# Key, query and gate weights in one load each, zeros in threes, x reordered by a copy in memory: an AdaLN block with a delta-rule attention on one core

## The chip, the cores and the metric

The kernel runs on one core of one Trainium2 chip. The metric is the device time of one execution, in microseconds; the time of a kernel is the median of its runs. The profiled execution is one run of its own, taken by the hardware profiler, and its time is given beside the runs.

The names in the profile: PE is TensorE (PEld its weight loads), DVE is VectorE, ACT is ScalarE, POOL is GpSimd, SP is the engine that here only issues DMAs; SPq, PEq and so on are the issuing sides. L610 is line 610 of the kernel.

## What is computed

The block has two halves. The first is an attention without softmax over 4 sequences of 1024 tokens with 256 channels: 16 heads of 64, a causal convolution of 4 taps, and a state S of 64x64 per head and sequence that is carried from token to token. The second is a mixture of 8 experts of which every token takes 2. The reference, cut:

```python
q, k, v = (silu(causal_conv(x @ W.T)) for W in (Wq, Wk, Wv))      # 1024 channels
k = k / max(norm(k), 1e-12)                                        # per head
alpha, beta = sigmoid(x @ Wa.T + ba), sigmoid(x @ Wb.T + bb)
def step(S, xs):                                                   # token after token
    kt, vt, qt, at, bt = xs
    upd = vt - at * (S @ kt)
    S = clip(at * S + bt * outer(upd, kt), -5.0, 5.0)
    return S, S @ qt
out = (y * silu(x @ Wg.T + bg)) @ Wo.T

mod = (silu(c) @ wmod)                                             # six modulations
h = layernorm(x) * (1 + ca) + sa
x = x + ga * attention(h)
h = layernorm(x) * (1 + cb) + sb
x = x + gb * moe(h)                                                # top 2 of 8 experts
```

All arrays are float32.

## The kernel before

**Tiling.** The 1024 tokens of each sequence are cut into 32 chunks of 32 tokens; a chunk with all 4 sequences is 128 rows. Two chunks make a pair, and there are 16 pairs. Within a chunk the recurrence is solved in closed form (a triangular system per head), and S is carried from chunk to chunk. After the last pair, `blocks` runs the experts over blocks of 256 routed rows.

**What one turn of the main loop does** (`chunks`, lines 1505 to 1521). While the two chunks of pair g go through the passes with the state (`Chunk.passes`, L1098), pair g + 1 is prepared (`Pair`, from L640): rows and norms, decays, keys and queries, values and gates, the triangle, the scaling. Each of these is a generator, and the string `PLAN` says which generator takes its next step. So the order of the instructions on PE, DVE, ACT and POOL is written out by hand. SP's order is not: it is left to the scheduler, which places each DMA. Each engine works through its list in order; an instruction waits for semaphores, and all that stand behind it on its engine wait too.

**The instructions around the change, in the order in which data goes through them:**

- `load_kq` (L425): the weights of one head pair, a tile `w_kq` of keys and queries, by two DMAs of 128 KB on SP. `load_v` (L431): `w_v` by one DMA of 128 KB, and the gate's weights `w_gt` by two of 64 KB. They are called two head pairs ahead (L746, L771), and PE's projections L610 and L780 read them.
- `load_x` and `fill_x` (L417, L421): a chunk of x comes in an order (half, sequence, token) and is put into (sequence, half, token) by eight DMAs of 16 KB. `loads` (L1391) does this for two chunks a pair, three pairs ahead; the first two chunks are split between SP's and ACT's queues, and `later_loads` (L1472) fetches four more.
- `clear` (L1335): the rows in memory to which the routing will scatter are blanked, 132 KB (128 rows of 1056 bytes) by a DMA, in six steps of three a pair.
- `triangle` (L840): DVE turns the products of keys round (L871), takes from their diagonal the norms (`rk`, L874, L892) and from these and the decays the factors `spread` (L894, L895). SP stores them to `g_scratch` in memory (L900), four DMAs, one for each sequence's 32 partitions. Then DVE solves the triangular system: L920 and L926 for the blocks of 8, and for each of two halves L934, L941, L943, L948, L956. Of these L934, L943 and L948 are products of two operands in SBUF, L941 and L956 are reductions. Then Tt, Tn and r_r are turned (L962, L965, L967), and PE's L1019 reads Tn. In the plan, steps of other generators lie between: the routing (L541 to L583), the state's sum S (L1196), the projections' convolution (L628), the sum of the residual `add` (L1276).
- `scaled` (L978): four times (for keys w = 1 and for queries w = 0, and for both chunks `par`), SP loads a tile `sc` back from `g_scratch` by two DMAs, each of which broadcasts 4 KB to 64 partitions; POOL multiplies keys or queries by it in two instructions (L1001), and for the keys copies the last column to `last` (L1004). The four tiles share two buffers, which the triangle used before.
- POOL's list around it: the residual's sum x (L1278, which waits for DVE's L1276), the first multiply L1001, two indirect stores of the routing (L586, which wait for DVE's L583), `aS` (L1231, the state times its decay), two small copies into hT (L1070, L1091), the second multiply L1001, `last`, the third, `Tr` (L972), the fourth.
- DVE's S (L1196) reads `aS`; `yT` (L1252) follows S on DVE, and PE's next projection takes the bank that `yT` read.

The lines of the fan-out and of the read-back:

```python
for b, q in enumerate(quads):
    nc.sync.dma_start(g_dram[g][:, :, b].rearrange("w n t -> n w t"), spread[q])
...
def at_heads(g, w, p, par):
    n = p * 16 + par * 8
    return g_dram[g][w, n : n + 8].rearrange("n b t -> (n b t)")
```

Of the kernel before, what the change touches and what calls it, by code (L numbers as in the profile page):

```python
# [32 lines left out]
F32 = mybir.dt.float32  # L33
# [3 lines left out]
ALU = mybir.AluOpType  # L37
# [324 lines left out]
def chunks(ctx, tc, a, nch, con, ones, modt, modc, x1_dram, rt, out):  # L362
# [61 lines left out]

    def load_kq(hp):  # L425
        w = s3.tile([P, 2, 2, P], F32, name="w_kq")
        for x, i in ((KK, 0), (QC, 1)):
            nc.sync.dma_start(w[:, :, i], a["w_qkv"][:, :, x, hp])
        return w

    def load_v(hp):  # L431
        w = s3.tile([P, 2, P], F32, name="w_v", bufs=3)
        nc.sync.dma_start(w, a["w_qkv"][:, :, VC, hp])
        wg = s3.tile([P, 2, P], F32, name="w_gt", bufs=4)
        for p in range(2):
            nc.sync.dma_start(wg[:, :, half_p(p)], a["w_g"][:, :, p, hp * DH : (hp + 1) * DH])
        return w, wg
# [202 lines left out]
    class Pair:  # L640
# [100 lines left out]
        def keys_and_queries(self):  # L741
            need(("h", self.g), ("halo", self.g))
            kq = self.kq = take(s2, [P, 2, HP, 2, B, TC], "kq", bufs=2)
            for hp in range(HP):
# [3 lines left out]
                for x, i in ((KK, 0), (QC, 1)):  # L748
                    two.append(project(w[:, :, i], self.h_t, x, hp, kq[:, i, hp]))
                    yield  # L750
# [89 lines left out]
        def triangle(self):  # L840
# [58 lines left out]
            for b, q in enumerate(quads):  # L899
                nc.sync.dma_start(g_dram[g][:, :, b].rearrange("w n t -> n w t"), spread[q])  # L900
# [77 lines left out]
        def scaled(self):  # L978
# [11 lines left out]
            for w in (1, 0):  # L990
                for par in range(2):
                    sc = take(s1, [P, HP, B, TC], "sc", tag=("kk", "kk_r")[par])
                    for p in range(2):
                        nc.sync.dma_start(
                            sc[half_p(p)].rearrange("q h b t -> q (h b t)"),
                            at_heads(g, w, p, par).partition_broadcast(DH),
                        )
                    yield
                    for h4 in range(0, HP, 4):
                        o = kq[:, w, h4 : h4 + 4, par]  # L1000
                        nc.gpsimd.tensor_tensor(o, o, sc[:, h4 : h4 + 4], ALU.mult)  # L1001
                    if w == 1:
                        last = take(s3, [P, B, HP], "last", bufs=3)
                        nc.gpsimd.tensor_copy(last.rearrange("q b h -> q h b"), sc[:, :, :, TC - 1])  # L1004
# [43 lines left out]
    def at_heads(g, w, p, par):  # L1048

        n = p * 16 + par * 8  # L1050
        return g_dram[g][w, n : n + 8].rearrange("n b t -> (n b t)")
# [277 lines left out]
    g_dram = nc.dram_tensor("g_scratch", [npair, 2, 32, B, TC], F32, kind="Internal").ap()  # L1329
# [5 lines left out]
    def clear(count):  # L1335

        for _, (n, e) in zip(range(count), blank):
            one = nc.sync.dma_start(rows[n][:, e], rt.zero)
            for other in rt.sent:
                apart(tc, one, other)  # L1340
            blanks.append((n, one))
# [49 lines left out]
    def loads(first):  # L1391
        for c in range(first, min(first + 2, nch)):
            load_x(c)
# [78 lines left out]
    def later_loads():  # L1472
# [7 lines left out]
        nc.sync.dma_start(rw, a["router"])  # L1480
        for p in range(2):
# [925 lines left out]
```

## Time and profile before

| what | value |
|---|---|
| runs | 1910.82, 1913.59, 1915.36 us; median 1913.59 |
| profiled execution | 1922.9 us, its span from first to last instruction 1921.1 us |
| granted clock of TensorE | 0.919 over the span |
| PE by line | projections L610 of keys and queries 323.2 us, of values 153.5; gate L780 144.3; experts L2116 136.4 and L2129 130.3; output L1265 121.0 |
| POOL, L1001 | 163.5 us in 128 instructions; 143.6 us idle before them, of which 116.5 until an `sc` had landed |
| DMA | 431490 packets, 249.52 MB, mean 130 GB/s |

The page's groups name an operation with its line, what it writes and reads, how often, its busy time and mean, and the engine's idle time just before it with what ended that. The chain of waits is followed back from the last instruction: at each step to what released it. In a timeline each row is a start, a length, engine, line, operation, tiles, count, and in brackets the idle time before it and what ended it. A row that ends an idle time by "issue" waited for nothing that the profile shows.

### The profile page before, as it was taken

What the parts mean: (1) busy time and instruction counts of PE and PEld (TensorE: products, weight loads), DVE (VectorE), ACT (ScalarE), POOL (GpSimd) and SP (SyncE); (2) the same over time, 40 slices, a digit from 0 to 9 for tenths busy, and PEclk for the clock granted to TensorE, in tenths of its full rate; (3) what the DMA queues carried; (4) which work ended last, traced back from release to release, by engine and by line L of the source; (5) the groups of instructions that cost most, each with busy time, mean ns of one, the idle gap of its engine ahead of it and who ended that gap; (6) DMA issues with size and microseconds to landing.
All of it is one profiled execution on the core that took longest, in us unless ns stands there. A gap on an engine that the chain in (4) does not pass through costs nothing.

```text
span 1921.1 us, 88201 instructions
## 1 busy us (share of the span) xinstructions
PE 1632.0 (85%) x38610; PEld 1297.1 (68%) x38610; DVE 1482.3 (77%) x3622; ACT 826.7 (43%) x1652; POOL 716.4 (37%) x913
## 2 busy tenths in 40 slices
PE   5578999889989898989898989898888675989994
PEld 3456676667676766767676767676667564878883
DVE  4678797968788888878787978797968335789973
ACT  3344545444545544545445444554443112334331
POOL 1032343424342525252534343433424432454343
PEclk9889998989999998989899989998989677999997
DMA  4455444443545445354535453636343216788882
GB/s 117 127 161 129 105 108 94 107 109 95 148 115 141 123 120 137 107 134 111 146 103 150 106 153 97 161 94 153 110 112 112 56 36 207 187 208 219 231 231 35
DMA packets 431490, 249.52 MB, mean 130 GB/s; under 512 B 242996, under 2 KB 410808, under 8 KB 430840
## 3 DMA queue, kind: packets, MB, share of 16 engines
q1 hardware_dynamic: 416488, 223.65, 43.6%
q0 software_dynamic: 13664, 18.38, 5.2%
q8 instruction: 306, 5.01, 1.1%
q10 hardware_dynamic: 944, 1.77, 0.3%
q14 instruction: 88, 0.72, 0.1%
HBM read 165.99 MB, written 81.87 MB: 129 GB/s over the span
## 4 chain that ended last, share of the span: by engine, by line
PE 66%; DVE 11%; issue 7%; POOL 5%; SPq 5%; DMA 4%; ACT 3%; POOLq 0%; DVEq 0%; ACTq 0%
PE ps_q L610 22%; PE ps_hm L2116 6%; PE ps_yb L2129 6%; PE ps_w L1265 5%; PE ps_gt L780 4%; PE ps_u L1149 3%; PE ps_kk L853 3%; PE ps_o L1208 2%; PE ps_z L1127 2%; SPq L423 2%; PE ps_t L1031 2%; PE ps_s L1187 2%; DMA sc<-g_scratch 2%; PE ps_t L1019 2%; DVE kq L628 2%
## 5 line engine op out<-in xcount | busy, mean ns | idle before, releaser
L628 DVE SCALAR_TENSOR_TENSOR kq<-ps_q,w_conv,kq 128x256 f32<-128x256 f32 x768 | 319.7, 476 | 150.2 <-ACT kq L619 149.6
L610 PE MATMUL ps_q<-hT,w_kq 128*128 128x280 f32 x1024 | 323.2, 460 | 58.9 <-issue 20.6
L610 PEld LDWEIGHTS ps_q<-hT,w_kq 128*128 128x128 f32 x1024 | 203.5, 213 | 125.9 <-issue 58.2
L619 ACT ACTIVATE kq<-ps_q,w_conv 128x256 f32<-128x256 f32 x256 | 142.4, 563 | 234.8 <-PE ps_q L610 233.1
L1001 POOL TENSOR_TENSOR kq<-kq,sc 128x512 f32<-128x512 f32 x128 | 163.5, 1299 | 143.6 <-DMA sc<-g_scratch 116.5
L2136 POOL DMA_INDIRECT out<-yb,at_b x72 | 120.4, 1672 | 190.2 <-DVE gate L2106 48.7
L628 DVE SCALAR_TENSOR_TENSOR v<-ps_q,w_conv,v 128x256 f32<-128x256 f32 x384 | 158.9, 476 | 41.9 <-ACT v L619 41.7
L1231 POOL TENSOR_TENSOR aS<-S,last 128x1024 f32<-128x1024 f32 x64 | 122.5, 1914 | 135.9 <-DVE S L1196 133.4
L780 PE MATMUL ps_gt<-hT,w_gt 128*128 128x256 f32 x512 | 144.3, 410 | 29.6 <-issue 20.5
L787 ACT ACTIVATE gate<-ps_gt,b_gt 128x256 f32<-128x256 f32 x128 | 60.5, 473 | 239.3 <-PE ps_gt L780 239.1
L610 PE MATMUL ps_q<-hT,w_v 128*128 128x280 f32 x512 | 153.5, 441 | 11.6 <-issue 4.7
L2116 PE MATMUL ps_hm<-hT,w 128*128 128x256 f32 x576 | 136.4, 392 | 7.6 <-issue 5.9
L2123 ACT ACTIVATE hm<-ps_hm,b 128x256 f32<-128x256 f32 x144 | 68.2, 474 | 167.5 <-issue 120.4
L2129 PE MATMUL ps_yb<-w,hm 128*128 128x256 f32 x576 | 130.3, 379 | 0.0
L2116 PEld LDWEIGHTS ps_hm<-hT,w 128*128 128x128 f32 x576 | 112.7, 197 | 25.9 <-issue 8.9
L610 PEld LDWEIGHTS ps_q<-hT,w_v 128*128 128x128 f32 x512 | 97.7, 204 | 47.3 <-issue 13.1
L780 PEld LDWEIGHTS ps_gt<-hT,w_gt 128*128 128x128 f32 x512 | 92.0, 194 | 53.1 <-issue 28.5
L1265 PE MATMUL ps_w<-w_o,yT 128*128 128x256 f32 x512 | 121.0, 391 | 4.3 <-DVE yT L1252 2.8
L1278 POOL TENSOR_TENSOR x<-x,add 128x256 f32<-128x256 f32 x32 | 29.0, 905 | 236.4 <-DVE add L1276 232.3
L2129 PEld LDWEIGHTS ps_yb<-w,hm 128*128 128x128 f32 x576 | 106.7, 190 | 13.4 <-DVE yb L2134 0.3
L1265 PEld LDWEIGHTS ps_w<-w_o,yT 128*128 128x128 f32 x512 | 98.2, 195 | 20.1 <-DVE yT L1252 3.0
L619 ACT ACTIVATE v<-ps_q,w_conv 128x256 f32<-128x256 f32 x128 | 71.3, 573 | 93.7 <-PE ps_q L610 93.7
(265 smaller groups left out, 3230.5 us busy)
## 6 DMA issues: line engine op xcount, KB each, us to landing
w<-in_w SPq DMA_DIRECT2D x72, 512.0 KB
rows_scratch<-zero_row SPq DMA_DIRECT2D x272, 132.0 KB
w_kq<-in_w_qkv SPq DMA_DIRECT2D x260, 128.0 KB
sc<-g_scratch SPq DMA_DIRECT2D x128, 256.0 KB
w_v<-in_w_qkv SPq DMA_DIRECT2D x130, 128.0 KB
w_gt<-in_w_g SPq DMA_DIRECT2D x260, 64.0 KB
u_scratch<-u SPq DMA_DIRECT2D x128, 128.0 KB
hb<-rows_scratch SPq DMA_DIRECT2D x36, 264.0 KB
```

The costliest lines, as they stand in the source:

```text
L610: nc.tensor.matmul(ps.rearrange("p y t -> p (y t)"), lhsT=w[:, dc], rhs=h_t[:, dc].rearrange("p x b t -> p (x b t)"), start=(dc == 0), sto ...
L619: nc.scalar.activation(o, ps[:, :, 0:TC], AF.Identity, scale=taps[:, 0:1], bias=taps[:, KC : KC + 1])
L628: nc.vector.scalar_tensor_tensor(o, ps[:, :, j : j + TC], taps[:, j : j + 1], o, op0=ALU.mult, op1=ALU.add)
L780: nc.tensor.matmul(ps, lhsT=wg[:, dc], rhs=self.h_t[:, dc, :, :, KC - 1 :].rearrange("p x b t -> p (x b) t"), start=(dc == 0), stop=(dc == 1),
L787: nc.scalar.activation(gate[:, hp].rearrange("p x b t -> p (x b t)"), ps.rearrange("p y t -> p (y t)"), AF.Silu, bias=b_gt[:, hp : hp + 1],)
L1001: nc.gpsimd.tensor_tensor(o, o, sc[:, h4 : h4 + 4], ALU.mult)
L1231: nc.gpsimd.tensor_tensor(aS.rearrange("q b h i -> q (b h) i"), S[:, bs].rearrange("q b h i -> q (b h) i"), self.pair.last[self.par][:, bs ...
L1265: nc.tensor.matmul(ps_w, lhsT=self.yT[:, hp].rearrange("q b t -> q (b t)"), rhs=w_o[:, hp], start=(hp == 0), stop=(hp == HP - 1),)
L2116: nc.tensor.matmul(ps, lhsT=self.w1[:, dc, fc * P : (fc + 1) * P], rhs=self.hT[:, dc], start=(dc == 0), stop=(dc == 1),)
L2123: nc.scalar.activation(self.hm[:, fc], ps, AF.Gelu, bias=self.b1[:, fc : fc + 1])
L2129: nc.tensor.matmul(ps, lhsT=self.hm[:, fc, s * P : (s + 1) * P], rhs=self.w2[:, fc], start=(fc == 0), stop=(fc == 3),)
L2136: return nc.gpsimd.indirect_dma_start(out=places, out_offset=bass.IndirectOffsetOnAxis(ap=self.at[:, s : s + 1], axis=0), in_=y, in_offset ...
```

## The change

Six edits, none of them to what is computed:

- keys and queries of a head pair come in one DMA of 256 KB; the tile's two halves change places, and the projection takes its half by the index in the weights
- both halves of the gate's weights come in one DMA of 128 KB
- the blanks of one step that belong to the same chunk go in one DMA, up to three
- `spread` is stored by one DMA of 128 partitions; for this, `g_scratch` has the sequence ahead of the head, and an `sc` tile has it too: each partition gets four runs of 1 KB instead of one of 4 KB, and POOL reads `sc` in runs of 32 elements. `last` is written in the order in which it is read
- from chunk 6 on, x is put in order by a DMA from memory to memory (`reorder_x`, into `x_rows`), issued a pair before the load, which is then one DMA of 128 KB. The chunks 0 to 5 are loaded as before; the copies for 6 and 7 are issued in `later_loads`, ahead of the loads of `w_o`
- SP's list is placed anew by the scheduler, with all this

```diff
--- before.py
+++ after.py
@@ -422,18 +422,28 @@
         for there, here in by_batch(a["x"][c], x):
             eng.dma_start(here, there)
 
+    x_rows = nc.dram_tensor("x_rows", [nch, P, D], F32, kind="Internal").ap()
+
+    def reorder_x(c):
+
+        if 6 <= c < nch:
+            nc.sync.dma_start(
+                x_rows[c].rearrange("(b h t) d -> b h (t d)", b=B, h=2),
+                a["x"][c].rearrange("(h b t) d -> b h (t d)", b=B, h=2),
+            )
+
     def load_kq(hp):
         w = s3.tile([P, 2, 2, P], F32, name="w_kq")
-        for x, i in ((KK, 0), (QC, 1)):
-            nc.sync.dma_start(w[:, :, i], a["w_qkv"][:, :, x, hp])
+        nc.sync.dma_start(w, a["w_qkv"][:, :, : KK + 1, hp])
         return w
 
     def load_v(hp):
         w = s3.tile([P, 2, P], F32, name="w_v", bufs=3)
         nc.sync.dma_start(w, a["w_qkv"][:, :, VC, hp])
         wg = s3.tile([P, 2, P], F32, name="w_gt", bufs=4)
-        for p in range(2):
-            nc.sync.dma_start(wg[:, :, half_p(p)], a["w_g"][:, :, p, hp * DH : (hp + 1) * DH])
+        nc.sync.dma_start(
+            wg.rearrange("x c (p i) -> x c p i", p=2), a["w_g"][:, :, :, hp * DH : (hp + 1) * DH]
+        )
         return w, wg
 
     w_next, v_next = [], []
@@ -746,7 +756,7 @@
                 w_next.append(load_kq((hp + 2) % HP))
                 two = []
                 for x, i in ((KK, 0), (QC, 1)):
-                    two.append(project(w[:, :, i], self.h_t, x, hp, kq[:, i, hp]))
+                    two.append(project(w[:, :, x], self.h_t, x, hp, kq[:, i, hp]))
                     yield
                 convolve(*two)
                 yield
@@ -896,8 +906,7 @@
                 spread[:, 0], spread[:, 1], -1.0, rk, op0=ALU.mult, op1=ALU.mult
             )
 
-            for b, q in enumerate(quads):
-                nc.sync.dma_start(g_dram[g][:, :, b].rearrange("w n t -> n w t"), spread[q])
+            nc.sync.dma_start(g_dram[g].rearrange("w b n t -> (b n) w t"), spread)
             done.add(("spread", g))
             w_t = s1.tile([P, TC], F32, name="w_t")
             nc.vector.tensor_tensor(w_t, be, rk, ALU.mult)
@@ -989,19 +998,21 @@
             self.last = []
             for w in (1, 0):
                 for par in range(2):
-                    sc = take(s1, [P, HP, B, TC], "sc", tag=("kk", "kk_r")[par])
+                    sc = take(s1, [P, B, HP, TC], "sc", tag=("kk", "kk_r")[par])
                     for p in range(2):
                         nc.sync.dma_start(
-                            sc[half_p(p)].rearrange("q h b t -> q (h b t)"),
+                            sc[half_p(p)].rearrange("q b h t -> q b (h t)"),
                             at_heads(g, w, p, par).partition_broadcast(DH),
                         )
                     yield
                     for h4 in range(0, HP, 4):
                         o = kq[:, w, h4 : h4 + 4, par]
-                        nc.gpsimd.tensor_tensor(o, o, sc[:, h4 : h4 + 4], ALU.mult)
+                        nc.gpsimd.tensor_tensor(
+                            o, o, sc[:, :, h4 : h4 + 4].rearrange("q b h t -> q h b t"), ALU.mult
+                        )
                     if w == 1:
                         last = take(s3, [P, B, HP], "last", bufs=3)
-                        nc.gpsimd.tensor_copy(last.rearrange("q b h -> q h b"), sc[:, :, :, TC - 1])
+                        nc.gpsimd.tensor_copy(last, sc[:, :, :, TC - 1])
                         self.last.append(last)
                     close(("kk", "kk_r")[par])
                     if (w, par) == (0, 1):
@@ -1048,7 +1059,7 @@
     def at_heads(g, w, p, par):
 
         n = p * 16 + par * 8
-        return g_dram[g][w, n : n + 8].rearrange("n b t -> (n b t)")
+        return g_dram[g][w, :, n : n + 8].rearrange("b n t -> b (n t)")
 
     def of_pair(w, g):
 
@@ -1326,7 +1337,7 @@
             yield
 
 
-    g_dram = nc.dram_tensor("g_scratch", [npair, 2, 32, B, TC], F32, kind="Internal").ap()
+    g_dram = nc.dram_tensor("g_scratch", [npair, 2, B, 32, TC], F32, kind="Internal").ap()
 
     rows = rt.rows[: NE * rt.room].rearrange("(e n p) d -> n p e d", e=NE, p=P)
     blank = iter([(n, e) for n in range(nch + BL // P) for e in range(NE)])
@@ -1334,11 +1345,16 @@
 
     def clear(count):
 
-        for _, (n, e) in zip(range(count), blank):
-            one = nc.sync.dma_start(rows[n][:, e], rt.zero)
+        some = [at for _, at in zip(range(count), blank)]
+        for n in sorted({n for n, _ in some}):
+            es = [e for m, e in some if m == n]
+            k = len(es)
+            one = nc.sync.dma_start(
+                rows[n][:, es[0] : es[0] + k], rt.zero.unsqueeze(1).to_broadcast([P, k, RW])
+            )
             for other in rt.sent:
                 apart(tc, one, other)
-            blanks.append((n, one))
+            blanks.extend([(n, one)] * k)
 
     def clears():
         for _ in range(6):
@@ -1390,7 +1406,9 @@
 
     def loads(first):
         for c in range(first, min(first + 2, nch)):
-            load_x(c)
+            reorder_x(c + 2)
+            x_of[c] = take(s3, [P, D], "x", bufs=9)
+            nc.sync.dma_start(x_of[c], x_rows[c])
             yield
 
     def both_of(pair, prev):
@@ -1478,6 +1496,8 @@
             if c > 2:
                 yield
         nc.sync.dma_start(rw, a["router"])
+        for c in (6, 7):
+            reorder_x(c)
         for p in range(2):
             for x in range(2):
                 nc.sync.dma_start(
```

## Prediction

> **What bounds the kernel now.** I read the page first, then the chain of waits of one pair, then the timelines of SP, POOL, DVE and PE around one place of every pair. "Pair" is one pass of the main loop; pair g's place is where DVE finishes `spread` (L895) for pair g, called +0.
>
> ```profile
> PE 1632.0 (85%) x38610; PEld 1297.1 (68%) x38610; DVE 1482.3 (77%) x3622; ACT 826.7 (43%) x1652; POOL 716.4 (37%) x913
> PE 66%; DVE 11%; issue 7%; POOL 5%; SPq 5%; DMA 4%; ACT 3%; POOLq 0%; DVEq 0%; ACTq 0%
> ```
>
> PE sets the time, and SP's queue (SPq) is on the chain with 5% of 1921.1 us, 96 us; of that L423, the loads of x, has 2% alone. That share is what the change aims at. The timelines of pair 7 (+0 is 723.85) show where it comes from:
>
> ```profile
> 723.88 1.75 SPq L900 DMA_DIRECT2D g_scratch<-spread  x4
> 730.50 5.49 SPq L423 DMA_DIRECT2D x<-in_x  x8
> 736.03 1.13 SPq L994 DMA_DIRECT2D sc<-g_scratch  x2
> ...
> 733.25 1.11 POOL L1278 TENSOR_TENSOR x<-x,add 128x256 f32<-128x256 f32 x1
> 740.71 2.71 POOL L1001 TENSOR_TENSOR kq<-kq,sc 128x512 f32<-128x512 f32 x2 [6.36 <-PE ps_q L610]
> 746.15 1.92 POOL L1231 TENSOR_TENSOR aS<-S,last 128x1024 f32<-128x1024 f32 x1
> ...
> 750.07 4.07 PE L610 MATMUL ps_q<-hT,w_kq 128*128 128x280 f32 x8 [1.17 <-DVE yT L1252]
> ```
>
> Between the store of `spread` and the `sc` loads that read it back, SP issues 14 other loads (736.03 - 725.63 = 10.4 us). So `sc` is issued at +12.2 and POOL multiplies at +16.9, though it was free at +10.5 (end of L1278). Behind that multiply, in POOL's order, stand two indirect stores, `aS`, the copies into hT, and the second multiply; `aS` feeds DVE's S (L1196), then yT, then PE. But a late `sc` costs PE little: the idle before L610 that yT ends is 0 to 2.8 us, over the pairs 4 to 13 13.95 us in all. DVE is busy without a break from 716 to 747 there and is late by itself.
>
> The same place has a second face. In pairs 3 and 14 little stands between `spread` and `sc`, which is issued at +5.8. Pair 14 (+0 is 1365.37):
>
> ```profile
> 1371.17 2.42 SPq L994 DMA_DIRECT2D sc<-g_scratch  x4
> ...
> 1376.19 3.19 POOL L1001 TENSOR_TENSOR kq<-kq,sc 128x512 f32<-128x512 f32 x2 [0.33 <-DMA sc<-g_scratch]
> 1382.48 1.90 POOL L1231 TENSOR_TENSOR aS<-S,last 128x1024 f32<-128x1024 f32 x1
> 1384.63 2.48 POOL L1001 TENSOR_TENSOR kq<-kq,sc 128x512 f32<-128x512 f32 x2
> ...
> 1376.30 2.00 DVE L948 TENSOR_TENSOR prod<-T,X 128x512 f32<-128x512 f32 x1
> 1382.28 4.92 DVE L943 TENSOR_TENSOR X<-X,rk 128x64 f32<-128x64 f32 x1
> 1387.23 1.01 DVE L948 TENSOR_TENSOR prod<-T,X 128x512 f32<-128x512 f32 x1
> ...
> 1391.02 2.05 PE L780 MATMUL ps_gt<-hT,w_gt 128*128 128x256 f32 x4 [5.19 <-issue]
> ...
> L943 DVE TENSOR_TENSOR X<-X,rk x32: 224/225/4920, 96.6 to 1484.7; 128x64 f32<-128x64 f32 x32
> ```
>
> POOL comes early and works beside DVE's L934 to L956. There L948 takes 2.00 us (1.04 is its median) and L943 4.92 (0.225): it starts at 1382.28, just before `aS`, and ends at 1387.20, when POOL's row of `aS`, two hT copies and both multiplies is over. Tn then comes at +27.8 instead of +22.3, and PE stands idle for 5.19 us. The starts of L895 give the price: 452.43 to 1365.18 is 91.28 us a pair over pairs 4 to 13 (late `sc`); 351.15 to 452.43 is 101.28 (pair 3), 1365.18 to 1465.40 is 100.22 (pair 14). So an early `sc` made a pair 8.9 to 10.0 us longer, twice of twice.
>
> **The change part by part.** The four compute engines keep every instruction and its place in the built program; SP's list alone changes, and DMA sizes.
>
> *Merged weights, zeros, spread.* w_kq 260 to 130 issues, w_gt 260 to 130, zeros 272 to 113, spread 64 to 16; x from 248 to 40 plus 26 copies in memory and 26 loads. In pairs 4 to 13 SP is occupied 680 of 913 us, at 0.5 to 0.9 us an issue by line; about 40 issues fewer a pair frees some 25 us of SP. By itself this is worth nothing: outside the two places below nobody waits for SP (by the waits no weight load ends a wait of PE after the first pair). Bytes of weights and zeros, and their runs, stay. The copy adds 128 KB read and written 26 times, 6.7 MB on 249.5; DMA is half busy: 0.
>
> *Start.* PE waits 7.05 us at 53.34 for w_kq of the sixth head pair, whose issue starts at 46.25 behind an SP queue full from 0.75 on. Ahead of it the change drops 5 w_kq and 4 w_gt issues and adds 2 copies: 9 x 0.6 - 2 x 0.68 (the price of the like copy at L1283) = 4.0 us. The two copies move 256 KB ahead of it, at the 230 GB/s of busy stretches 1.1 us: -3, bounds -4 to 0.
>
> *sc comes early in every pair.* Between spread and the first `sc` SP now has 1 to 4 single issues (up to 6 in pair 7) in place of 14. Issue of spread at +0.1, 0.5 us; three issues at 0.6; pair 1 issued `sc` 2.4 us after the last spread store without waiting for it: `sc` goes out at about +3.1. It was landed 4.5 to 4.9 us after issue in pairs 7 and 14, so +8 (+10 if the copy and x ahead cost another 2). POOL's order holds the multiply behind L1278, which ends at +10.5 in every pair because DVE's add (L1276) is at +8.9. So the multiply starts at +10.5: the place of pairs 3 (+10.7), 14 (+10.8) and 15 (+10.5). From there both engines run from the same event: the store L586 waits for DVE's L583; `aS` starts 2.86 us after L583 and L943 2.66 us after it, in pair 3 as in pair 14. Same gap, same stall. For pairs 4 to 13: 10 x 8.9 (pair 14, the lower and the one next to them) = +89. Bounds: below, DVE's own loss 0.9 + 4.7 less the removed yT wait 1.4 = 4.2 a pair, +42, since the rest of the 8.9 is a PE gap of 3.3 us in L1019 and a cold clock (PEclk 0.50 at 1388 to 1394) that other DMA timing could spare; above, 10.0 plus 0.9 for L943 being caught by the first multiply too, as in pair 15: +109. Pair 2 (sc at +7.5 today, 89.0 us) becomes like pair 1 (90.5): +1.5. Pairs 3, 14, 15 are early already.
>
> The Trainium skill, "SBUF — State Buffer", section "Who interferes with whom", says that a DVE instruction with two SBUF inputs and a GpSimd instruction that reads SBUF exclude each other, one blocking the other for one whole instruction. That speaks against this change; but by it L943 would lose one `aS`, 1.9 us, not 4.7, and the ten pairs only 0.9 + 1.9 - 1.4 = 1.4 each, 1926 us in all. The rows go by the whole train.
>
> The Trainium skill, "DMA: Bandwidth & Descriptors", section "Rules for kernel authors", wants many small transfers made one large; by it the 96 us of SPq would be the prize, 1818 us. The chain's share is no prize, since DVE stands 1 to 3 us behind it.
>
> *sc in another order.* A tile lands as 512 runs of 1 KB instead of 128 of 4 KB; zeros with runs of 1056 B and weights with 512 B move at the same 220 to 350 GB/s as `sc`: 0. POOL reads runs of 32 elements: L972 with runs of 16 takes 1.06 us for 512 elements, less than the 1.27 of L1001; the worst row, L1278 alone (0.73 for 256), would make it 1.46. From 0 to +0.2 per multiply, of which two a pair lie in the train: taken 0, up to +6 in all.
>
> **Sum.** -3 + 89 + 1.5 = +87.5 on the profiled execution (1922.9; its span 1921.1). The median of the runs is 1913.6, 9 us (0.5%) lower, so 1913.6 + 87.5 = 2001. Own range: -4 + 42 to +109 + 1.5 + 6, less for all worst at once: 1950 to 2020.
>
> **Rivals.**
> 1. *The engines take turns.* POOL comes early, but as in pairs 1 and 15 L943 and L948 lose 0.9 each, twice, because L943 falls into a gap of POOL's row: 3.6 - 1.4 = 2.2 a pair, +22 - 3 + 1.5: 1934. For: pair 15, same start of POOL. Against: there DVE's S waited 1.28 us for a PE that had stalled, and the hT copies were missing, so the phase was another.
> 2. *Faster.* `sc` lands only after +12, behind the copy, past L948; the train then falls on PSUM-reading L628 and transposes, as today. The yT waits go: -14 - 3 = 1897, lower if PE's clock stays up there (0.50 from 750 to 759 in pair 7, up to 4.9 us a pair). It decides if the landing takes over 8.5 us after issue; the rows say 4.5 to 4.9.
> 3. *Nothing*: both effects vanish, since PE's other work covers them: 1914. Against: 5.19 us of PE idle in pair 14 was not covered.
>
> **How the numbers follow.** Forecast 0.64 (2001), taking turns 0.13 (1934), faster 0.18 (1897), nothing 0.05. About 0.2% is what a measurement tells from no change. Faster 0.18, same 0.05, slower 0.77. The range 1905 to 2018 holds the forecast's and rivals 1 and 3, and leaves out most of the faster case and a little on top; the forecast's own is 1950 to 2020.
>
> **What would show it.** `sc` issued near +3 and the first multiply at +10.5 in pairs 4 to 13; L943 with about 14 long calls of near 4.9 us instead of 2, its mean of 637 ns near 2000; pairs of 100 us by L895; PE idle of some 5 us at L780; SPq gone from the chain, DVE's share up. Wrong if L943 stays at 0.23 with early multiplies (then rival 1 or 2), if the multiply starts after +12, or if pairs lengthen with L943 short, which would put the cost on DMA. The start is right if w_kq of the sixth head pair ends PE's wait near 50.

## The result and the profile after

The changed kernel takes 1998.5 us (median of 4 runs, 1995.4 to 2005.1), the kernel before 1913.7: a ratio of 1.0449, with a 95% interval of 1.0417 to 1.0482. The forecast was 2001. The profiled run of after took 2005.13 us with a span of 2003.3, that of before 1922.90 with 1921.1. A few executions, here and in the runs below, fell in a slower state of the chip, and as the ratios leave these out, a ratio need not be the quotient of two medians.

The page of after, with the engines' busy time, the chain's shares and TensorE's gate matmuls:

```profile
PE 1663.1 (83%) x38610; PEld 1322.6 (66%) x38610; DVE 1548.0 (77%) x3622; ACT 828.1 (41%) x1652; POOL 722.9 (36%) x913
...
PE 69%; DVE 13%; issue 10%; ACT 4%; DMA 2%; POOL 1%; SPq 0%; POOLq 0%; DVEq 0%; ACTq 0%
...
L790 PE MATMUL ps_gt<-hT,w_gt 128*128 128x256 f32 x512 | 153.8, 432 | 70.1 <-issue 61.0
```

The gate matmuls and the product X*rk of before:

```profile
L780 PE MATMUL ps_gt<-hT,w_gt 128*128 128x256 f32 x512 | 144.3, 410 | 29.6 <-issue 20.5
...
L943 DVE TENSOR_TENSOR X<-X,rk 128x64 f32<-128x64 f32 x32 | 20.4, 637 | 1.1
```

SP's queue has left the chain: 5% is now 0%. But DVE rose from 11% to 13%, "issue" from 7% to 10%, and the gate matmuls (L790, L780 before) are preceded by 70.1 us of idle time instead of 29.6. TensorE executes the same 38,610 matmuls and is busy 31 us longer, at a granted clock of 0.901 instead of 0.919. VectorE is busy 65.7 us longer, also for the same instructions. Most of it, 54.8 us (75.2 against 20.4), is one group of 32 small products. This is its row in the groups of DVE (busy us, mean ns, idle before):

```profile
L952 DVE TENSOR_TENSOR X<-X,rk 128x64 f32<-128x64 f32 x32 | 75.2, 2350 | 1.1
```

The timeline of pair 7 of after shows how it came. +0, the end of `spread` on DVE, is 750.05; columns are start, duration, engine, line:

```profile
750.08 0.37 SPq L909 DMA_DIRECT2D g_scratch<-spread  x1
...
754.39 1.29 SPq L1003 DMA_DIRECT2D sc<-g_scratch  x2
...
760.53 2.48 POOL L1010 TENSOR_TENSOR kq<-kq,sc 128x512 f32<-128x512 f32 x2
...
760.73 1.13 DVE L952 TENSOR_TENSOR X<-X,rk 128x64 f32<-128x64 f32 x1
...
761.90 1.94 DVE L957 TENSOR_TENSOR prod<-T,X 128x512 f32<-128x512 f32 x1
...
767.82 4.90 DVE L952 TENSOR_TENSOR X<-X,rk 128x64 f32<-128x64 f32 x1
...
768.01 1.92 POOL L1242 TENSOR_TENSOR aS<-S,last 128x1024 f32<-128x1024 f32 x1
...
770.16 2.47 POOL L1010 TENSOR_TENSOR kq<-kq,sc 128x512 f32<-128x512 f32 x2
...
772.59 0.22 POOL L1015 COPY last<-sc 128x32 f32<-128x32 f32 x1
772.76 1.02 DVE L957 TENSOR_TENSOR prod<-T,X 128x512 f32<-128x512 f32 x1
...
776.56 2.05 PE L790 MATMUL ps_gt<-hT,w_gt 128*128 128x256 f32 x4 [4.07 <-issue]
```

`sc` is issued at +4.3 (before: +12.2) and the multiply starts at +10.5 (before: +16.9). The second L952 starts 0.2 us ahead of `aS` and ends 0.04 us before L957, while GpSimd copies `last`. What GpSimd runs meanwhile is called the train below: `aS`, two copies into hT (not shown here), and the two instructions of the second multiply, without a gap between them. TensorE then stands idle for 4.07 us at L790. Tn, the turned triangle that PE's L1030 reads, comes at +28.7 in nearly every pair, 22.3 before.

Where the 82.2 us between the two spans lie, by the ends of `spread` (end of L905 to L907, L895 before):

```
stretch                         before    after   difference
start to the first spread         87.1     88.9        +1.8
pairs 0 to 2                     264.3    266.0        +1.7
pair 3                           101.3    104.2        +2.9
pairs 4 to 13                    912.8    978.3       +65.5
pair 14                          100.2    101.6        +1.4
last spread to the end           455.5    464.3        +8.8
```

### The profile page after: what moved, and what is told of

It is laid out like the page before. It is cut to its first block, busy times and chain, and to the rows that moved or that the text cites. A ratio compares the mean times of both kernels' runs of the same rounds, so it can differ in the third digit from the quotient of the medians.

```text
span 2003.3 us, 87456 instructions
## 1 busy us (share of the span) xinstructions
PE 1663.1 (83%) x38610; PEld 1322.6 (66%) x38610; DVE 1548.0 (77%) x3622; ACT 828.1 (41%) x1652; POOL 722.9 (36%) x913
## 2 busy tenths in 40 slices
DMA packets 445988, 252.84 MB, mean 126 GB/s; under 512 B 232716, under 2 KB 433296, under 8 KB 445136
## 4 chain that ended last, share of the span: by engine, by line
PE 69%; DVE 13%; issue 10%; ACT 4%; DMA 2%; POOL 1%; SPq 0%; POOLq 0%; DVEq 0%; ACTq 0%
PE ps_q L620 20%; PE ps_hm L2136 6%; PE ps_gt L790 6%; PE ps_yb L2149 6%; PE ps_w L1276 5%; PE ps_o L1219 3%; PE ps_s L1198 3%; PE ps_kk L863 3%; PE ps_u L1160 2%; PE ps_t L1030 2%; DVE v L638 2%; PE ps_o L1178 2%; PE ps_t L1042 2%; DVE kq L638 2%; PE ps_y L1258 2%
## 5 line engine op out<-in xcount | busy, mean ns | idle before, releaser
L620 PE MATMUL ps_q<-hT,w_kq 128*128 128x280 f32 x1024 | 318.3, 454 | 47.4 <-issue 17.0
L620 PEld LDWEIGHTS ps_q<-hT,w_kq 128*128 128x128 f32 x1024 | 201.0, 210 | 115.1 <-issue 47.9
L1010 POOL TENSOR_TENSOR kq<-kq,sc 128x512 f32<-128x512 f32 x128 | 161.5, 1281 | 145.1 <-DMA sc<-g_scratch 133.5
L790 PE MATMUL ps_gt<-hT,w_gt 128*128 128x256 f32 x512 | 153.8, 432 | 70.1 <-issue 61.0
L638 DVE SCALAR_TENSOR_TENSOR v<-ps_q,w_conv,v 128x256 f32<-128x256 f32 x384 | 159.2, 477 | 30.0 <-ACT v L629 28.7
L790 PEld LDWEIGHTS ps_gt<-hT,w_gt 128*128 128x128 f32 x512 | 97.4, 206 | 96.7 <-issue 73.3
L620 PE MATMUL ps_q<-hT,w_v 128*128 128x280 f32 x512 | 149.3, 430 | 13.5 <-issue 5.1
L620 PEld LDWEIGHTS ps_q<-hT,w_v 128*128 128x128 f32 x512 | 95.6, 200 | 46.9 <-issue 12.9
L596 POOL DMA_INDIRECT rows_scratch<-row_h,at x64 | 66.2, 1035 | 123.8 <-DVE at L593 112.6
```

The costliest lines, as they stand in the source:

```text
L596: one = nc.gpsimd.indirect_dma_start(out=rt.rows, out_offset=bass.IndirectOffsetOnAxis(ap=at[:, k : k + 1], axis=0), in_=line, in_offset=None,
L620: nc.tensor.matmul(ps.rearrange("p y t -> p (y t)"), lhsT=w[:, dc], rhs=h_t[:, dc].rearrange("p x b t -> p (x b t)"), start=(dc == 0), sto ...
L638: nc.vector.scalar_tensor_tensor(o, ps[:, :, j : j + TC], taps[:, j : j + 1], o, op0=ALU.mult, op1=ALU.add)
L790: nc.tensor.matmul(ps, lhsT=wg[:, dc], rhs=self.h_t[:, dc, :, :, KC - 1 :].rearrange("p x b t -> p (x b) t"), start=(dc == 0), stop=(dc == 1),
L1010: nc.gpsimd.tensor_tensor(o, o, sc[:, :, h4 : h4 + 4].rearrange("q b h t -> q h b t"), ALU.mult)
```

## The experiments

Twelve kernels were run. The kernel before, run beside them, had medians of 1913.7 to 1928.7 us in the five comparisons, so ratios are compared here, each to the before of its own comparison. In the table, "pair" is the mean of pairs 4 to 13, "long X" counts the products X*rk of 4.6 us or more, `sc` and "multiply" are the first issue and the first multiply in pairs 4 to 13, and "issue" sums TensorE's idle time of that name between the first and the last spread. These columns are worked out from each run's one trace; ratio and interval come from its other executions too. The ranges that are given in us were set with before at 1914 to 1916 us. In the comparison of `held_old_rows`, `old_rows`, `broken_train` and `before_held` it took 1928.7, and their times are to be read with that: on a before of 1913.7 their ratios make 1894, 1974, 1949 and 1890 us.

```
run                 ratio   95% interval      pair  long X  sc           multiply      issue
before              1                         91.3    2     +11.0..13.1  +16.3..19.0    90.8
after               1.0449  1.0417 to 1.0482  97.8   11     +2.9..4.7    +10.5..10.8   159.0
held_multiply       1.0200  1.0143 to 1.0257  94.2    0     +2.7..5.0    +16.3..21.4   119.7
x_after_factors     1.0172  1.0116 to 1.0229  92.1    2     +6.2..7.8    +11.5..13.8   107.3
x_alone             1.0040  1.0004 to 1.0077  92.2    1     +5.8..10.3   +11.8..17.1   102.8
all_but_x           1.0375  1.0287 to 1.0462  97.0    6     +3.1..6.7    +10.5..12.1   122.7
held_old_rows       0.9898  0.9866 to 0.9930  90.9    0     +3.8..6.6    +16.3..19.7    95.8
old_rows            1.0316  1.0263 to 1.0368  97.0   11     +4.2..6.8    +10.5..12.5   149.2
broken_train        1.0184  1.0156 to 1.0211  95.6    0     +3.0..5.1    +10.5..11.1   137.8
before_held         0.9876  0.9837 to 0.9914  90.3    0     +11.4..13.3  +16.4..19.5    86.2
held_new_rows       0.9926  0.9885 to 0.9967  91.0    0     +8.2..11.5   +16.3..18.0   103.5
rows_2k             0.9966  0.9917 to 1.0014  92.0    0     +3.5..6.2    +16.3..21.3   107.6
weights_zeros_held  0.9908  0.9864 to 0.9952  92.5    0     +5.0..7.1    +16.3..20.0    97.4
all_but_x_held      1.0193  1.0152 to 1.0234  95.0    0     +2.8..7.1    +16.3..20.4   114.2
```

### held_multiply: the early multiply taken out of the way

On the changed kernel, the product X*rk is remembered and the first multiply waits for it. The steps of the plan that emit the second X*rk and this multiply are placed ahead of the step that emits `aS`, and both tiles' loads of w = 1 are emitted ahead of both multiplies. On PE, DVE and ACT the order of instructions is unchanged; on GpSimd the multiply now stands behind the indirect stores and ahead of `aS`. SP's list differs in places.

```diff
-                nc.vector.tensor_tensor(
+                self.solved = nc.vector.tensor_tensor(
                     X, X, rk[:, at[1]].unsqueeze(1).to_broadcast([P, TE, TE]), ALU.mult
...
+                        if (w, par, h4) == (1, 0, 0):
+                            behind(tc, one, self.solved)
```

> The changed kernel with all its transfers kept; only the first multiply by the factors (tile 1 of w=1) is put behind the second half's X*rk on VectorE, and so after the two indirect stores and ahead of aS on GpSimd. Theory (the early multiply draws the train of aS, two hT copies and two multiplies under X*rk): the second X*rk of pairs 3 to 15 falls from 4.9 us to 0.23, Tn goes back from +28.7 to about +22.3, and the whole pair 3 and pair 14 are freed too, which stalled already before the change; time 1890 to 1915. Rival (the larger transfers themselves cost it, by their places on the queue, their sizes or the other layout of sc): the X*rk may fall, but pairs stay at 97 to 100 us and the time within 15 us of 1998.

Measured: 1956.8 us, ratio 1.0200. A miss for both. Every X*rk is short, in the view of tile X of this run (min, median, max in ns):

```profile
L952 DVE TENSOR_TENSOR X<-X,rk x32: 224/224/227, 95.7 to 1511.5; 128x64 f32<-128x64 f32 x32
```

About half of the loss is gone with the stall, 1.0449 to 1.0200; the other half has another cause. The pairs still take 94.2 us and TensorE's "issue" is 119.7 us instead of 90.8. Its place is inside groups of small matmuls. TensorE's timeline in pair 9 of this run:

```profile
957.56 1.03 PE L1036 MATMUL ps_t<-Tn,kd 32*32 32x16 f32 x100
962.41 0.61 PE L1036 MATMUL ps_t<-Tn,kd 32*32 32x16 f32 x28 [3.83 <-issue]
```

A group of 128 matmuls, started 10 ns apart, stops after 100 for 3.83 us, with no wait that the profile names. The DMA view of the half microsecond 959.5 to 960 of that pause:

```profile
DMA packets 171, 0.18 MB, mean 361 GB/s; under 512 B 3, under 2 KB 170, under 8 KB 170
...
q8 instruction: 1, 0.02, 17.1%
```

A packet of an instruction queue moves in the pause, amid 361 GB/s of data (130 is the mean of before). The trace settles whose packet it is: queue q8 moved 306 packets of 16,384 bytes in this run, one for every 255 of TensorE's 77,940 recorded instructions, and no other engine has 4,000. The pauses also stand at one place of TensorE's program. Between the first and the last spread, 38 of its idle times named "issue" last over 1 us. If its instructions are counted from the start of the trace, 35 of the 38 end at number 193 or 194 of a run of 256, each 1.2 to 1.5 us after a packet of q8 had landed; the other three are at L790 and L620. So at this place TensorE waits for its next block of code. Its idle times of over 0.15 us there sum to 51.5 us in before, 89.9 in after and 93.1 in this run. The stall shows in the rest: of after's 46 pauses of over 1 us, 13 (54.3 us) are not at this place, all of them at L790 and L620; before has 5 (19.3 us), at L780 and L610.

That data in flight make the code late isn't shown: the 35 pauses have 81 GB/s at the median and the 3 us ahead of each 193, where the time from the first to the last spread has 121 on the mean. The Trainium skill, "Runtime: NRT & Kernel Launch", section "Instruction fetch mechanics", says that an engine loads its code in blocks of 16 KiB over a queue of its own, with the cost mostly hidden. The size of the packets agrees; 93.1 us of waits aren't hidden.

### x_after_factors, x_alone, all_but_x: which edit brings the factors forward

`x_after_factors` changes no transfer of the kernel before; one letter of the plan, the second x, moves behind the step that loads the factors:

```diff
-...ctzctttcvchvvxhccctccvctstrt...
+...ctzctttcvchvvhccctccvctsxtrt...
```

> The kernel before with no transfer changed in size or number: the eight loads of a tile of x are only emitted after the first loads of the factors instead of ahead of them, so that these are issued near +6 in pairs 4 to 13 instead of +11 to +13. Theory: the multiply starts at +10.7 to +11.3, the second X*rk takes 4.9 us in most of pairs 4 to 13 as it does in pairs 3 and 14 of before, those pairs take 98 to 101 us, and the time is 1980 to 2005, with none of the edits made. Rival (size, layout or number of transfers): nothing but the order on SP moves, and the time stays within 15 us of 1914.

Measured: 1948.1 us (1931.3 to 1956.5), ratio 1.0172. The multiply came at +11.5 to +13.8, not at +10.7 to +11.3, and only pairs 14 and 15 have the long X*rk; both theories miss. The profiled run was the fastest of the four, so its trace shows less than the median lost. So the median's loss is not explained by this trace. What it does tell is where the stall ends: in pairs 3 to 14, here or in `old_rows`, no product takes 4.9 us where the multiply starts at +12.1 or later, and in `old_rows` all eleven pairs where it starts at +11.8 or earlier have one. The limit isn't sharp: in `all_but_x` pair 5 has one of 4.97 us with the multiply at +12.11, and here pair 4, at +11.52, has none.

`x_alone` is the kernel before with the functions of the copy of x (its definition and the copies for chunks 6 and 7 are as in the change, and left out here):

```diff
...
-            load_x(c)
+            reorder_x(c + 2)
+            x_of[c] = take(s3, [P, D], "x", bufs=9)
+            nc.sync.dma_start(x_of[c], x_rows[c])
...
```

> The kernel before with the edit of x alone: a copy in memory and one load for each tile in place of eight loads. The queue issues nine transfers fewer ahead of the factors but three zeros more, so the factors are issued near +9 (four spread stores, three zeros, six weights, two of x at 0.55 to 0.6 us) and the multiply starts near +14. Theory: it stands half way: the multiply meets the second X*rk or T*X but not the train of aS, X*rk takes 0.5 to 1.1 us, T*X 1.9, 1 to 3 us a pair, 1915 to 1945. Rival (the copy in memory itself costs what the change lost): about 1990.

Measured: 1928.6 us, ratio 1.0040, inside the range. `sc` came at +9.3 to +10.3 in pairs 4 to 12, the multiply mostly near +16: this edit alone doesn't bring the stall (one long product, in pair 13, where the kernel before has two).

`all_but_x` is the changed kernel without that edit (the same lines in reverse).

> The changed kernel with x loaded by eight transfers a tile as before, everything else merged. One spread store, one or two weights and five loads of x stand ahead of the factors, so these are issued near +4.5 and the multiply still starts at +10.5 behind the x-add. Theory: X*rk is held 4.9 us in nearly all of pairs 3 to 15, 1985 to 2005; so the weights, zeros and spread alone bring the loss without x. Rival (the copy of x is what costs): back within 15 us of 1914.

Measured: 1995.8 us, ratio 1.0375, as the theory had it in time. In the count it is only half right: six products of 4.6 us or more, four of 2.2 and one of 3.98. The merged weights, zeros and spread bring most of the loss without x.

### held_old_rows, old_rows: the layout of the factors

Both undo, on the changed kernel, the single store of `spread` and the layout of `sc`. A tile of factors lands again as one row of 4 KB for each partition, not four of 1 KB. `held_old_rows` keeps the multiply held, `old_rows` does not.

```diff
-            nc.sync.dma_start(g_dram[g].rearrange("w b n t -> (b n) w t"), spread)
+            for b, q in enumerate(quads):
+                nc.sync.dma_start(g_dram[g][:, :, b].rearrange("w n t -> n w t"), spread[q])
...
-                            sc[half_p(p)].rearrange("q b h t -> q b (h t)"),
+                            sc[half_p(p)].rearrange("q h b t -> q (h b t)"),
```

> The changed kernel with the multiply held behind X*rk (as in the run held_multiply, 1957 us) and, beside that, the store of spread and the loads of the factors as before the change: four stores of spread, and rows of 4 KB for a partition instead of four of 1 KB. In held_multiply X*rk took 0.22 us in every pair, yet TensorE's idle time named issue was 119.7 us between the first and the last spread, against 90.8 before the change, most of it inside the groups of 64 to 128 small matmuls that compute ps_t, ps_kk and ps_o. Theory A (the rows of 1 KB: about 14,500 packets more than before in all, so that the code which TensorE reads comes late): issue falls to 85 to 100 us and the time to 1905 to 1930. Theory B (it is the place of the loads, early in the pair, or the other merges, and not the rows): issue stays at 110 to 130 and the time at 1945 to 1965.

> The changed kernel with only the store of spread and the layout of the factors as before the change (four stores, rows of 4 KB). The factors are issued near +5, the multiply still starts near +10.5 behind the x-add. Theory of the prediction (the early multiply alone): X*rk is held 4.9 us in most of pairs 3 to 15 and the time stays 1980 to 2005. Rival (the rows of 1 KB cost what the change lost): 1915 to 1945.

Measured: `held_old_rows` 1911.3 us, ratio 0.9898, issue 95.8, as theory A said. `old_rows` 1986.7 us, ratio 1.0316, 11 long products, as the early multiply alone said in us and in the count; by its ratio the time is below that range. So each alone gives back a part (1.0449 to 1.0316, 1.0449 to 1.0200), and both together give back all of it. TensorE's groups of `held_multiply`, busy us, mean ns, idle before:

```profile
L1225 PE MATMUL ps_o<-u,dq 32*32 32x64 f32 x4096 | 88.6, 229 | 11.8 <-issue 11.5
...
L1036 PE MATMUL ps_t<-Tn,kd 32*32 32x16 f32 x4096 | 49.7, 187 | 47.3 <-issue 29.8 <-ACT ab_r L715 15.2 <-DVE r_r L976 2.3
```

The same two groups in `held_old_rows`:

```profile
L1226 PE MATMUL ps_o<-u,dq 32*32 32x64 f32 x4096 | 80.8, 224 | 5.8 <-issue 5.5
...
L1037 PE MATMUL ps_t<-Tn,kd 32*32 32x16 f32 x4096 | 48.4, 186 | 39.1 <-issue 21.8 <-ACT ab_r L715 13.0 <-DVE r_r L977 2.1
```

The pauses fall from 11.5 to 5.5 and from 29.8 to 21.8 us, and ps_o is also busy 7.8 us less. From the first to the last spread `held_multiply` takes 38.9 us longer than `held_old_rows`. Of these, 16.4 are waits for code, counted as above (93.1 against 76.7), and 14.5 are TensorE busy longer with the same matmuls (1228.8 against 1214.3), at a granted clock of 0.928 instead of 0.943. The second X*rk of `held_multiply` comes at +17 to +21 instead of +16 in six of pairs 4 to 13. In five of them a pause of 1 to 3.4 us at ps_s or ps_o, between +10 and +14, goes ahead: S waits for ps_s, and X*rk stands behind S in DVE's order. In pair 5 the profile doesn't name what S waited for.

The two terms overlap. Without the stall the rows of 1 KB cost 94.2 - 90.9 = 3.3 us a pair; beside the stall 97.8 - 97.0 = 0.8. With rows of 4 KB the stall costs 97.0 - 90.9 = 6.1 us a pair.

### broken_train: what X*rk waits for

The changed kernel, with the second tile's first multiply behind X*rk, so that nothing follows the hT copies at once:

```diff
+                        if (w, par, h4) == (1, 1, 0):
+                            behind(tc, one, self.solved)
```

> The changed kernel with the first multiply where it is (early), but the second tile's first multiply put behind the second X*rk, so that GpSimd's train ends after aS and the two hT copies. Theory (X*rk waits for a gap on GpSimd's train, not for one instruction): X*rk falls from 4.9 us to what is left of aS and the copies, 2.2 to 2.4 us, 2.5 us a pair in some 12 pairs: 1960 to 1980. Rival 1 (it waits for one instruction only and its length has another cause): X*rk stays at 4.9. Rival 2 (the stall of VectorE hides behind TensorE's own gaps): X*rk falls, the time stays within 8 us of 1998.

Measured: 1963.4 us, ratio 1.0184; the long product is 2.19 us. Pair 8 of this run:

```profile
846.27 2.19 DVE L952 TENSOR_TENSOR X<-X,rk 128x64 f32<-128x64 f32 x1
...
846.46 1.92 POOL L1244 TENSOR_TENSOR aS<-S,last 128x1024 f32<-128x1024 f32 x1
848.30 0.23 POOL L1083 COPY hT<-hT 128x24 f32<-128x24 f32 x1
848.49 0.20 POOL L1104 COPY hT<-hT 128x24 f32<-128x24 f32 x1
...
848.65 3.19 POOL L1010 TENSOR_TENSOR kq<-kq,sc 128x512 f32<-128x512 f32 x2
```

The product ends at 848.46, with `aS` over and the first copy ending, and the multiply, which now starts behind it, no longer falls under it. Shortening the train by two multiplies shortened the product by 2.7 us, so the train theory holds and both rivals fall. To the instruction the records don't show what lets the product go: it ends 0.2 us before the second copy does, and in after it ends while `last` is copied. The time follows: the span is 42.9 us below that of after (1960.4 against 2003.3), 22 of it in pairs 4 to 13, 8.6 in pair 3 and 9.9 behind the last spread. Of these 9.9 the product of pair 15, 2.5 us shorter, can account for a part; the rest is open.

### before_held: the kernel before without its two stalls

The hold of `held_multiply` on the kernel before.

> The kernel before with its transfers as they are, and the first multiply put behind the second X*rk and behind the indirect stores (as in held_multiply). Theory: pairs 3 and 14, the only ones of before with X*rk at 4.9 us, lose that; nothing else moves, since in pairs 4 to 13 the multiply came later by itself: 1895 to 1912, 3 to 9 us of a gain for each of the two pairs. Rival (those two pairs are long because their factors are loaded early among other transfers, not by X*rk): 1910 to 1920.

Measured: 1904.5 us, ratio 0.9876: 24 us below its own before. Pair 3 falls from 101.3 to 92.3 us and pair 14 from 100.2 to 94.6, as predicted; the other pairs gain 1.0 us each on the mean, which was not expected. So the 24 us are more than the 2 to 19 that the range meant, and of the 21.9 us between the two spans only 14.6 lie in the two pairs. This is the lowest ratio of all kernels here, and it has none of the merges; the intervals of `held_old_rows`, `weights_zeros_held` and `held_new_rows` overlap with its own.

### held_new_rows, rows_2k, weights_zeros_held, all_but_x_held: what the rows meet

`held_new_rows` is `before_held` with the single store of `spread` and rows of 1 KB (the diff of `held_old_rows` in reverse). `rows_2k` is `held_old_rows` with two rows of 2 KB for each partition (of its diff only the array is shown):

```diff
-    g_dram = nc.dram_tensor("g_scratch", [npair, 2, 32, B, TC], F32, kind="Internal").ap()
+    g_dram = nc.dram_tensor("g_scratch", [npair, 2, 2, 32, 2, TC], F32, kind="Internal").ap()
```

`weights_zeros_held` is `before_held` with only the weights and the zeros merged. `all_but_x_held` is `held_multiply` with x by eight loads.

> The kernel before with the multiply held (as before_held, 0.9876 of before) and, of the change, only the store of spread in one and the factors in rows of 1 KB; the order of transfers on SP is that of before_held but for three stores of spread fewer. Theory (rows of 1 KB make TensorE's code late): issue rises from 86 to 100 to 115 us, and the ratio to before from 0.988 to 1.005 to 1.02. Rival (the rows cost only together with the other merges, or it was the place of the loads): ratio within 0.98 to 0.995, issue within 10 us of 86.

> The changed kernel with the multiply held and the factors in two rows of 2 KB for a partition: half way, by size, between held_multiply (four of 1 KB, ratio 1.02, issue 120 us) and held_old_rows (one of 4 KB, ratio 0.99, issue 96 us); spread by four stores. Theory (the number of packets sets it: 8,192 more than with 4 KB, where 1 KB has 24,576 more): a third of the way, ratio 0.995 to 1.005, issue 100 to 108. Rival (it is a threshold on the size of a row, or the number of stores of spread): ratio at one of the two ends.

> The kernel before with the multiply held and, of the change, only the weights in one and the zeros by threes; x by eight loads, spread and the rows of the factors as before. The start is shorter by the weights (the first spread came at 82.7 us in all_but_x, 87.1 before and 92.4 in x_alone), so 4 us less than before_held there. Theory (with the train out of the way and rows of 4 KB, larger transfers cost nothing in a pair): ratio 0.983 to 0.990. Rival (larger weights or zeros hold TensorE up by themselves): 0.995 or more.

> The changed kernel with the multiply held, rows of 1 KB, merged weights and zeros, and x by eight loads a tile. Rows of 1 KB cost 0.5% without the other merges (held_new_rows 0.993 against before_held 0.988) and 3% with all of them (held_multiply 1.020 against held_old_rows 0.990). If the copy of x in memory is what they meet: ratio 0.990 to 1.000 and issue at 95 to 108 us. If it is the larger weights and zeros: ratio 1.010 to 1.020 and issue at 112 to 122. In between, both.

Measured. `held_new_rows` 1908.8 us, 0.9926: issue rose by 17 us to 103.5 as the theory had it, but the time hardly (its interval meets that of `before_held`), so rows of 1 KB alone cost some 0.5%, not clear of noise, and the theory's time missed. `rows_2k` 1922.2 us, 0.9966, issue 107.6: between 0.9898 and 1.0200 and in the range for a count of packets; but its interval, 0.9917 to 1.0014, overlaps with that of `held_old_rows`, so a threshold isn't excluded. `weights_zeros_held` 1908.5 us, 0.9908, issue 97.4: slightly above its range, with an interval that covers the range: the merged weights and zeros, with rows of 4 KB, are worth nothing measurable. `all_but_x_held` 1965.0 us, 1.0193, issue 114.2: as without x, so the copy of x isn't what the rows meet. TensorE's waits for code, counted as above, are 60.6 us in `before_held`, 76.4 in `held_new_rows`, 78.1 in `weights_zeros_held`, 90.6 in `rows_2k` and 89.2 in `all_but_x_held`: rows of 1 KB lengthen them, larger weights and zeros do so too, and the time doesn't follow them one to one (one trace each). What stays open is whether rows of 1 KB cost 3% because they are loaded early (+3 to +7, where `held_new_rows` has +8 to +11.5) or because larger weights and zeros run beside them; in these runs the two came together.

## Why the prediction was right, and where it was not

**The mechanism: right.** `sc` was issued at +2.9 to +4.7 and the multiply started at +10.5 to +10.8 in all of pairs 4 to 13, as worked out. X*rk was caught and held through GpSimd's train: 11 products of 4.6 us or more, 14 forecast; mean 2350 ns, "near 2000" forecast. In pairs 13 and 14 it wasn't held so long: there the second multiply came at +24.0 and +22.5 instead of +20.1, and X*rk took 1.08 and 2.14 us. The pairs 4 to 13 took 97.8 us, 100 forecast. SP left the chain, DVE's share rose, TensorE stood idle at L790. `broken_train` shows the train as the cause of the long product, `held_multiply` that the stall is worth about half of the loss when it alone is removed. The other half the prediction had at 0.

**The rule on shared SBUF.** By the Trainium skill, "SBUF — State Buffer", section "Who interferes with whom", the block lasts one whole instruction. With 4.90 us under `aS`, two copies and two multiplies, and 2.19 under `aS` and a copy, the runs decide against one instruction: the block grew and shrank with the train.

**The price of a pair: too high.** The prediction's +89, "10 x 8.9", is the term that was mis-sized: it measured +65.5, 6.5 a pair. The 8.9 was the difference of pair 14 to pairs 4 to 13, taken as if the stall were all that set them apart. `before_held` shows that it isn't: without any stall pairs 3 and 14 still take 92.3 and 94.6 us, where the others take 90.3, so 2 to 4 us belonged to those pairs anyway (one trace each).

**The layout of `sc` taken at 0: wrong.** "zeros with runs of 1056 B and weights with 512 B move at the same 220 to 350 GB/s as `sc`: 0" looked at the rate of the transfer alone. The runs put the rows of 1 KB with their single store of `spread` at 1.3% (1.0449 against 1.0316) beside the stall and 3.0% (1.0200 against 0.9898) without it. Of the 38.9 us between the traces behind the 3.0%, TensorE's waits for code and its longer busy time at a lower clock make 30.9. The third multiply also starts later with these rows (+30.8 against +27.0 at the median of pairs 4 to 13); whether that costs time wasn't tested. For GpSimd's own reading the 0 was right: its multiplies took 161.5 us against 163.5.

**The sum: near by luck.** On the profiled execution +87.5 was forecast, and the spans differ by 82.2. The ten pairs gave 23.5 us less than their +89, and stretches from which less was expected gave some 18 us back: 4.8 at the start, 4.3 in pairs 3 and 14, 8.8 behind the last spread. And of the 84.8 us between the medians, about 24 came with the layout that was taken at 0, since `old_rows` has a ratio of 1.0316, 60 us on 1913.7.

**The start of -3: wrong.** It measured +1.8, and the sign shown to be expected, an end of TensorE's wait for w_kq near 50, did not come. The wait of after:

```profile
52.93 2.21 PE L620 MATMUL ps_q<-hT,w_kq 128*128 128x280 f32 x4 [5.79 <-DMA w_kq<-in_w_qkv]
```

Before it ended at 53.34. In `all_but_x`:

```profile
48.64 1.18 PE L610 MATMUL ps_q<-hT,w_kq 128*128 128x280 f32 x4 [1.94 <-DMA w_kq<-in_w_qkv]
```

and in `x_alone`:

```profile
55.51 2.20 PE L620 MATMUL ps_q<-hT,w_kq 128*128 128x280 f32 x4 [8.87 <-DMA w_kq<-in_w_qkv]
```

The merged weights bring this wait's end 4.7 us forward, near the 5.4 counted (9 x 0.6), and the first spread of `all_but_x` comes at 82.7 instead of 87.1. The two copies of x ahead of it cost 52.93 - 48.64 = 4.3 us beside the merged weights, and 55.51 - 53.34 = 2.2 in `x_alone`, where 1.4 of issue and 1.1 of moving were counted. What made the first spread 1.8 us later than before, when this wait ended 0.4 us earlier, stays open.

**Not in the sum.** Pair 3 was 2.9 us longer, and the stretch behind the last spread 8.8. In the other runs that stretch took 454 to 466 us without following any one edit, so no cause is named for it.

**The rivals.** Turns of 0.9 us are what pair 13 did, and no other of pairs 4 to 13. "Faster" named the right limit, a multiply after +12, and `x_after_factors` sits on it; but its price was wrong, since neither that run (1.0172) nor `x_alone`, with the multiply mostly near +16 (1.0040), was faster. "SPq's 96 us are the prize", which the rule on coalescing in the Trainium skill, "DMA: Bandwidth & Descriptors", section "Rules for kernel authors", would have, is answered by `weights_zeros_held`, 0.9908 against 0.9876 with no merge at all, and for the loads of x by `x_alone`, 1.0040.

## What to carry to other kernels

A queue that is late can be what keeps two engines apart: before a transfer is made earlier, look at what its consumer will then run beside, and whether the kernel already contains places where that happens (here pairs 3 and 14). Such a place gives a price, but compare it with the same place with the cause removed, not with its neighbours. A wait that fixes the order of the two engines gave 1.2% here (`before_held`), and no merge showed a gain on top of it.

## What the runs showed of the hardware that was not expected

A VectorE product of two SBUF operands, which had started 0.2 us ahead of GpSimd's `aS`, stayed held through five GpSimd instructions without a gap, 4.90 us for 0.22 us of work, and was let go at 2.19 us when the train ended early. TensorE paused for up to 5.3 us in the middle of groups of small matmuls (`all_but_x_held`), and the pauses of over 1 us are not spread at random: of those named "issue" between the first and the last spread, 35 of 38 in `held_multiply` end at instruction 193 or 194 of a run of 256, and 21 of 26 in before, where TensorE waits for a packet of code. With rows of 1 KB (23,808 packets more for the same bytes: 445,988 against 422,180 in `held_old_rows`) these waits are longer, not more frequent: 93.1 us in 64 against 76.7 in 69. And for the same 38,610 matmuls TensorE was busy 31 us longer in after, at a granted clock of 0.901 instead of 0.919. That its idle time brings the lower clock isn't shown: behind the pause at L790 in pair 7 of after the clock is 0.83 and 0.66 over two stretches of 10 us, but before, without that pause, has 0.57 and 0.94 at nearly the same place of its pair 7 (751 to 771).
